# Causal attention: mask and row maximum of the scores in one VectorE call per head and query chunk, with a mask row over all keys

## The chip, the cores and the metric

The kernel runs on one core of a Trainium2 chip. The metric is device time in microseconds (us) of one execution of the whole program, lower being better. The engines are named as in the profile: PE (TensorE matmuls), PEld (TensorE weight loads), DVE (VectorE), ACT (ScalarE), POOL (GpSimd), SP (SyncE, which issues the DMAs).

## The reference, cut to what matters

The program is a stack of six blocks on a tensor of 16 sequences x 512 positions x 256 channels: a quantised feed-forward block, a Mamba block, the feed-forward block again, a LoRA expert block, **causal attention with ALiBi**, and the LoRA block again. Only the attention is touched:

```python
q = (x @ Wq + bq).reshape(Bb, Ss, H, HD)          # 16 heads of 16
k = (x @ Wk + bk).reshape(Bb, Ss, H, HD)
v = (x @ Wv + bv).reshape(Bb, Ss, H, HD)
scores = jnp.einsum('bthd,bshd->bhts', q, k) / jnp.sqrt(jnp.asarray(HD, x.dtype))
scores = scores + alibi[None]
scores = jnp.where(causal[None, None], -jnp.inf, scores)
attn = jax.nn.softmax(scores, axis=-1)
out = jnp.einsum('bhts,bshd->bthd', attn, v).reshape(Bb, Ss, Dd)
return out @ Wo + bo
```

## The kernel before, in words

The attention computes every score twice. First with queries on the partitions, only to find each query's maximum (the "peak" pass); then with keys on the partitions and the maximum already subtracted, to exponentiate (the "weigh" pass). ALiBi and the subtracted maximum ride in extra rows of the 32-row operands `q` and `k` of a head, so both passes are matmuls of 32 rows.

The work is cut into 64 **units** (16 sequences b x 4 groups j of 4 heads), and a unit into 6 **steps** (part, pair): three parts of query chunks (chunk 3 of 512 keys; chunk 2 of 384 keys; chunks 1 and 0 together, of 256 and 128 keys) times two pairs of heads. I number them step 0 to step 5; steps 0 and 1 are part 0, steps 2 and 3 part 1, steps 4 and 5 part 2. The loop over units (from L1564) is a software pipeline: while unit A goes through its peak pass, unit C (the one before) goes through its weigh pass and unit Dn (two before) is multiplied with the values. In each step:

- `peak_score` (L1170) and `weigh_score` (L1215) put the matmuls on PE, in turns. The scores of A land in a PSUM tile `s` with tag `sp`, of which there are two: step n+2 writes where step n was read.
- `weigh_exp` (L1233): ACT exponentiates the scores of C, POOL zeroes the masked triangle.
- `peak_max` (L1186): DVE adds the mask to the diagonal blocks of both heads of the pair (L1192, one TENSOR_TENSOR in PSUM), and then takes the maximum over the keys of each query chunk for both heads (L1196, one TENSOR_REDUCE for a chunk: one in parts 0 and 1, two in part 2). Results go into columns of `mx`.
- In step 0 of the next unit `peak_rows` (L1201) lets PE transpose `mx` (four 128x128 transposes, recorded at L1068) and DVE adds the result to `q`, giving `qm` (L1212), which the weigh pass of that unit needs from step 1 on. Then PE does `apply` (matmuls `o`).
- Between the steps `aside` (L1328) slips in side work: the projections of the coming sequence (`project`, L1070: norm at L1091 to L1100, the key bias on DVE at L1131 as `ku`, the values at L1154 and the output bias at L1164), the division (L1273, L1274) and the output projection (`close`, L1304).

Matmuls and transposes of this phase are kept in program order on PE (`keep_in_program_order`, L1065 and L1068). The DVE instructions are not: a scheduler places them, with semaphores for what depends on what, so an edit can move neighbours of the edited instruction too.

The mask is a bf16 tile of 128 x 256, two copies of one 128 x 128 triangle (L1037 to L1044), built once, before the first unit.

Of the kernel before, what the change touches and what calls it, by code (L numbers as in the profile page):

```python
# [10 lines left out]
BF16 = mybir.dt.bfloat16  # L11
AF = mybir.ActivationFunctionType
ALU = mybir.AluOpType
AX = mybir.AxisListType
PSUM = bass.MemoryType.PSUM

P = 128
NB, SEQ, D = 16, 512, 256
# [12 lines left out]
NX = NE * NR + 1  # L31
EPS = 1e-5
MASKED = -1e30


@with_exitstack
def macaron_kernel(
# [31 lines left out]
    nc = tc.nc  # L69

    const = ctx.enter_context(tc.tile_pool(name="const", bufs=1))
# [869 lines left out]
    def attn_phase(weights, pre):  # L941
# [8 lines left out]
        RS, RM = HD, HD + 1  # L950
# [10 lines left out]
        PEAK = (((3, 0),), ((2, 0),), ((1, 0), (0, 2 * P)))  # L961
        WEIGH = ((0,), (1,), (2, 3))
        wp, qs, ks, mxs, vas, qms, const, pools = {}, [], [], [], [], {}, {}, {}

        def constants(aw):

            for name, w in (("q", Wq), ("k", Wk), ("v", Wv), ("o", Wo)):
                t = aw.tile([P, KD, D], F32, name=f"w{name}")
                nc.sync.dma_start(out=t, in_=w.rearrange("(k p) f -> p k f", p=P))
                wp[name] = t  # L970
            bvb = aw.tile([P, D], F32, name="bvb")
            nc.sync.dma_start(out=bvb, in_=bv.unsqueeze(0).to_broadcast([P, D]))
            bob = aw.tile([P, D], F32, name="bob")
            nc.sync.dma_start(out=bob, in_=bo.unsqueeze(0).to_broadcast([P, D]))

            yield
            bq_t = aw.tile([P, KD], F32, name="bq_t")
            nc.sync.dma_start(out=bq_t, in_=bq.rearrange("(k p) -> p k", p=P))
            nc.vector.tensor_scalar(bq_t, bq_t, 0.25, None, op0=ALU.mult)
            bk_t = aw.tile([P, KD], F32, name="bk_t")  # L980
            nc.sync.dma_start(out=bk_t, in_=bk.rearrange("(k p) -> p k", p=P))

            prow = aw.tile([P, 1], F32, name="prow")
            nc.gpsimd.iota(
                prow, pattern=[[0, 1]], base=0, channel_multiplier=1,
                allow_small_or_imprecise_dtypes=True,
            )
            for i in range(1, 4):
                rows = prow[32 * i : 32 * i + 32, :]
                nc.vector.tensor_scalar(rows, rows, -32.0 * i, None, op0=ALU.add)  # L990
            is_s = aw.tile([P, 1], F32, name="is_s")
            nc.vector.tensor_scalar(is_s, prow, float(RS), None, op0=ALU.is_equal)
            neg_m = aw.tile([P, 1], F32, name="neg_m")
            nc.vector.tensor_scalar(
                neg_m, prow, float(RM), -1.0, op0=ALU.is_equal, op1=ALU.mult
            )
            slope = aw.tile([P, NJ], F32, name="slope")
            for h in range(NH):
                i, j = h % 4, h // 4
                nc.vector.memset(  # L1000
                    slope[32 * i : 32 * i + 32, j : j + 1], 2.0 ** (-8.0 / NH * (h + 1))
                )
            nc.vector.tensor_scalar(slope, slope, is_s, None, op0=ALU.mult)
            pos = aw.tile([P, SEQ], F32, name="pos")
            nc.gpsimd.iota(
                pos, pattern=[[1, SEQ]], base=0, channel_multiplier=0,
                allow_small_or_imprecise_dtypes=True,
            )


            yield
            for i in range(2):
                for j in range(NJ):
                    qs.append(aw.tile([P, SEQ], F32, name=f"q{i}{j}"))
                    ks.append(aw.tile([P, SEQ], F32, name=f"k{i}{j}"))
            last = ks[-1]
            nc.vector.tensor_scalar(last, pos, 0.0, neg_m, op0=ALU.mult, op1=ALU.add)
            for c, i, row in BLOCKS:
                nc.vector.tensor_scalar(
                    last[:, P * c + 32 * i : P * c + 32 * i + 32],  # L1020
                    prow.to_broadcast([P, 32]), float(row), neg_m,
                    op0=ALU.is_equal, op1=ALU.add,
                )
            yield
            for i in range(2):
                for j in range(NJ):
                    nc.vector.tensor_scalar(
                        qs[i * NJ + j], pos, 0.0, is_s, op0=ALU.mult, op1=ALU.add
                    )
                    nc.vector.scalar_tensor_tensor(  # L1030
                        ks[i * NJ + j], pos, slope[:, j : j + 1], last,
                        op0=ALU.mult, op1=ALU.add,
                    )
                    yield


            mask = aw.tile([P, 2 * P], BF16, name="mask")  # L1037
            nc.vector.memset(mask, 0.0)
            for i in range(2):
                square = mask[:, i * P : (i + 1) * P]  # L1040
                nc.gpsimd.affine_select(
                    out=square, in_=square, compare_op=ALU.is_ge,
                    fill=MASKED, base=0, pattern=[[-1, P]], channel_multiplier=1,
                )  # L1044
            yield
            for r in range(3):
                if r < 2:
                    mx = aw.tile([P, NC4, 4, 32], F32, name=f"mx{r}")
                    nc.gpsimd.memset(mx, 0.0)
                    for c, i, row in BLOCKS:  # L1050
                        nc.gpsimd.memset(mx[: 32 * i, c, :, row : row + 1], MASKED)
                    mxs.append(mx)
                va = aw.tile([P, NC4, VW], F32, name=f"va{r}")
                nc.gpsimd.memset(va, 1.0)
                vas.append(va)
            const.update(
                bvb=bvb, bob=bob, bq_t=bq_t, bk_t=bk_t, mask=mask
            )
# [126 lines left out]

        def peak_max(b, j, part, pair, s):  # L1186
            mx = mxs[(b * NJ + j) % 2]
            t, off = PEAK[part][0]
            w = len(PEAK[part]) * P

            own = s[:, :, off + t * P : off + t * P + w]
            nc.vector.tensor_tensor(  # L1192
                own, own, const["mask"][:, :w].unsqueeze(1).to_broadcast([P, 2, w]), op=ALU.add
            )
            for t, off in PEAK[part]:
                nc.vector.tensor_reduce(  # L1196
                    mx[:, t, 2 * pair : 2 * pair + 2, RM],
                    s[:, :, off : off + (t + 1) * P], axis=AX.X, op=ALU.max,
                )

        def peak_rows(b, j):  # L1201

# [104 lines left out]
        with tc.tile_pool(name="aw", bufs=1) as aw:  # L1307
            with tc.tile_pool(name="a", bufs=2) as ap, tc.tile_pool(
                name="a_s", bufs=1, space=PSUM
# [237 lines left out]


                making = constants(aw)
                for _ in range(2):  # L1550
                    rows_of.append(ap.tile([P, 4, EW], F32, name="eT", tag="eT"))
# [12 lines left out]
                for u in range(len(units) + 2):  # L1564
# [16 lines left out]
                    for n, (part, pair) in enumerate(steps):  # L1581
# [15 lines left out]
                        if A:  # L1597
                            peak_max(*A, part, pair, sp)
# [39 lines left out]
    with tc.tile_pool(name="mw", bufs=1) as mw:  # L1638
        with tc.tile_pool(name="x", bufs=1) as xp, tc.tile_pool(
            name="fw", bufs=1  # L1640
# [23 lines left out]
    with tc.tile_pool(name="fw2", bufs=1) as fw, tc.tile_pool(  # L1664
        name="ln2", bufs=2
    ) as lnp:
        weights = []
        for i, d in enumerate(kept):
            w = fw.tile([P, d.shape[1], d.shape[2]], F32, name=f"wk{i}")
# [66 lines left out]
```

## Time and profile before

| what | value |
|---|---|
| median of 3 runs (lowest, highest) | 4259.38 us (4258.01, 4263.89) |
| span of the profiled execution, first to last instruction | 4259.0 us |
| busy over the span: PE, DVE, ACT, POOL | 92%, 88%, 54%, 44% |
| mask and maximum on DVE (first L1192 to last L1196) | from 3126.7 to 4127 us of the span |
| mask additions L1192 | 384 instructions, 199.0 us |
| maxima L1196 | 512 instructions, 410.2 us on the page (421.1 us with all forms told apart) |
| mean granted PE clock | 0.975 |

The span is the time of the profiled execution as far as the profile has it; it lies 0.4 us under the median of the runs. A row of instructions gives the line, engine and operation, the tiles written and read, the shape (partitions x elements), the count, the busy time in us, and the mean of one in ns. In a list by time, the first number is the start in us from the start of the span and the second the duration. Two VectorE instructions in a row with no semaphore between them can overlap in such a list, since a record runs from an instruction's start to the end of its last write. The chain of waits follows the last instruction of the span backwards: at each point it holds the instruction that everything after was waiting for.

### The profile page before, as it was taken

How to read it: one execution, taken by the hardware profiler on the slowest of the kernel's cores; microseconds unless marked ns; L12 is line 12 of the kernel's file. 1: busy time of each engine (PE TensorE's matmuls, PEld its weight loads, DVE VectorE, ACT ScalarE, POOL GpSimd, SP SyncE). 2: the span in 40 equal slices, each digit the busy share in tenths (PEclk: the TensorE clock that was granted, in tenths of full speed). 3: DMA queues.
4: the chain of work that ended last, by engine and by line, in shares of the span. 5: the costliest groups of instructions: out<-in, count | busy, mean ns of one | idle time of the engine just before them, and what ended most of it. 6: DMA issues, size and time to landing. Idle time of an engine off the chain costs nothing.

```text
span 4259.0 us, 50441 instructions
## 1 busy us (share of the span) xinstructions
PE 3903.6 (92%) x17986; PEld 2129.9 (50%) x17986; DVE 3751.8 (88%) x4970; ACT 2284.9 (54%) x3463; POOL 1877.2 (44%) x1653
## 2 busy tenths in 40 slices
PE   6999977988899888888888799999999999999989
PEld 4676632333333333333333366666755555555547
DVE  9999858999999999999999899998878888888766
ACT  4444336667767676676777344443524444444434
POOL 1000027888888898888988600000301111111121
PEclk9999999999999999999999999999999999999999
DMA  4000023444444444444443020000000000000002
GB/s 143 16 16 15 20 100 104 132 122 134 139 144 144 144 143 144 134 135 133 139 138 120 11 109 1 1 1 1 13 21 20 19 17 18 19 20 14 21 11 70
DMA packets 120605, 303.00 MB, mean 71 GB/s; under 512 B 25297, under 2 KB 45330, under 8 KB 103970
## 3 DMA queue, kind: packets, MB, share of 16 engines
q1 hardware_dynamic: 120354, 299.78, 22.4%
q8 instruction: 142, 2.33, 0.2%
q14 instruction: 109, 0.89, 0.1%
HBM read 238.63 MB, written 44.30 MB: 66 GB/s over the span
## 4 chain that ended last, share of the span: by engine, by line
PE 66%; DVE 14%; POOL 12%; ACT 5%; issue 2%; DMA 1%; SPq 0%; DVEq 0%; POOLq 0%; ACTq 0%
PE y L486 11%; PE s L1065 10%; PE g L288 7%; PE u L288 7%; POOL bx L480 7%; PE o L324 7%; PE p L486 5%; PE p L1065 4%; DVE h L876 4%; PE o L486 3%; PE p L1068 3%; PE o L1065 3%; POOL g L480 2%; PE r L1065 2%; DVE mx L1196 2%
## 5 line engine op out<-in xcount | busy, mean ns | idle before, releaser
L480 POOL TENSOR_TENSOR bx<-dtu,bc 128x1024 f32<-128x1024 f32 x512 | 1193.9, 2360 | 46.4 <-DVE h L876 46.3
L486 PE MATMUL y<-g,ident 128*128 128x512 f32 x2048 | 1008.9, 631 | 128.7 <-DVE g L483 128.6
L876 DVE TENSOR_TENSOR_SCAN h<-da,bx 128x1024 f32<-128x1024 f32 x384 | 879.8, 2291 | 67.8 <-ACT da L477 30.4
L477 ACT ACTIVATE da<-dt,a_neg 128x511 f32<-128x511 f32 x1024 | 702.9, 688 | 219.3 <-DVE hs L876 116.8
L486 PEld LDWEIGHTS y<-g,ident 128*128 128x128 f32 x2048 | 390.0, 199 | 711.4 <-issue 464.8
L1242 POOL TENSOR_SCALAR_AFFINE_SELECT eT<-eT 128x256 f32<-128x256 f32 (+1 forms) x384 | 189.0, 492 | 867.0 <-ACT eT L1236 867.0
L1236 ACT ACTIVATE eT<-s 128x768 f32<-128x768 f32 (+1 forms) x384 | 338.4, 881 | 422.1 <-PE s L1065 422.1
L483 DVE TENSOR_TENSOR g<-h,bc 128x1024 f32<-128x1024 f32 x384 | 468.9, 1221 | 28.2 <-PE o L486 0.5
L1065 PE MATMUL s<-k,q 32*128 32x256 f32 (+3 forms) x2048 | 458.2, 469 | 9.1 <-DVE mx L1196 5.7
L1196 DVE TENSOR_REDUCE mx<-s 128x2 f32<-128x1024 f32 (+3 forms) x512 | 410.2, 822 | 12.5
L1065 PE MATMUL s<-qm,k 32*128 32x512 f32 (+3 forms) x2048 | 385.5, 471 | 18.2 <-ACT eT L1236 11.8
L480 POOL TENSOR_TENSOR g<-hs,bc 128x1024 f32<-128x1024 f32 x128 | 301.6, 2356 | 156.8 <-DVE hs L876 140.8
L1192 DVE TENSOR_TENSOR s<-s,mask 128x256 f32<-128x256 f32 (+1 forms) x384 | 199.0, 518 | 155.7 <-PE s L1065 145.6
L293 ACT ACTIVATE sl<-g 128x352 f32<-128x352 f32 x256 | 118.1, 464 | 383.2 <-PE g L288 372.4
L876 DVE TENSOR_TENSOR_SCAN hs<-da,bx 128x1024 f32<-128x1024 f32 x128 | 292.0, 2281 | 2.5 <-ACT da L477 2.5
L1065 PEld LDWEIGHTS s<-k,q 32*128 32x128 f32 x2048 | 205.7, 184 | 172.2 <-issue 93.8
L1393 POOL TENSOR_TENSOR g<-rs,v 128x4 f32<-128x4 f32 x64 | 13.1, 208 | 631.8 <-ACT rs L1390 548.8
L486 PE MATMUL p<-xT,w_in 128*128 128x512 f32 x500 | 242.1, 607 | 20.9 <-ACT xT L477 10.1
L509 POOL MEMSET xs<- 128x12 f32 x2 | 0.2, 110 | 532.7 <-DMA xd<-x 532.7
L477 ACT ACT_TABLE_LOAD x170 | 218.1, 1283 | 3.0
L1065 PEld LDWEIGHTS s<-qm,k 32*128 32x128 f32 x2048 | 170.1, 185 | 63.9 <-ACT eT L1236 34.7
L288 PE MATMUL g<-wgT,xT 128*128 128x352 f32 x512 | 183.7, 469 | 0.0
(270 smaller groups left out, 6766.6 us busy)
## 6 DMA issues: line engine op xcount, KB each, us to landing
bc<-bd SPq DMA_DIRECT2D x128, 1024.0 KB, 6.3
xs<-xc SPq DMA_DIRECT2D x240, 256.0 KB, 4.7
xc<-xp SPq DMA_DIRECT2D x60, 256.0 KB, 2.0
x<-_attn_hidden_states_dram SPq DMA_DIRECT2D x16, 512.0 KB, 6.6
xd<-x SPq DMA_DIRECT2D x16, 512.0 KB, 2.6
xo<-xd SPq DMA_DIRECT2D x16, 512.0 KB, 3.6
xe<-xo SPq DMA_DIRECT2D x16, 512.0 KB, 2.6
x<-xe SPq DMA_DIRECT2D x16, 512.0 KB, 10.7
```

The lines of the kernel that those rows point to most:

```text
L288: nc.tensor.matmul(dst, lhsT=xT[:, k, c * P : (c + 1) * P], rhs=w[:, k, f0 : f0 + HF], start=(k == 0), stop=(k == KD - 1),)
L324: last = nc.tensor.matmul(o, lhsT=hT[:, f, :], rhs=wdT[:, f, :], start=(f == 0), stop=False)
L477: return tc.keep_in_program_order(nc.scalar.activation(out, in_, func, **kw))
L480: tc.keep_in_program_order(nc.gpsimd.tensor_tensor(out, in0, in1, op=op))
L483: tc.keep_in_program_order(nc.vector.tensor_tensor(out, in0, in1, op=op))
L486: tc.keep_in_program_order(nc.tensor.matmul(out, **kw))
L876: tc.keep_in_program_order(nc.vector.tensor_tensor_scan(flat(h), flat(das[t % 2]), flat(bxs.pop(t)), 0.0, op0=ALU.mult, op1=ALU.add,))
L1065: tc.keep_in_program_order(nc.tensor.matmul(out, **kw))
L1192: nc.vector.tensor_tensor(own, own, const["mask"][:, :w].unsqueeze(1).to_broadcast([P, 2, w]), op=ALU.add)
L1196: nc.vector.tensor_reduce(mx[:, t, 2 * pair : 2 * pair + 2, RM], s[:, :, off : off + (t + 1) * P], axis=AX.X, op=ALU.max,)
L1236: const["exp"] = nc.scalar.activation(eT[:, 2 * pair : 2 * pair + 2, e0 : e0 + w], s[:, :, :w], AF.Exp)
L1242: nc.gpsimd.affine_select(out=own, in_=own, compare_op=ALU.is_ge, fill=0.0, base=0, pattern=[[0, 2], [0, n], [1, P]] if n > 1 else [[0, 2] ...
```

## The change

The mask becomes one bf16 row block of 128 x 512: zero everywhere but in the last 128 columns, which hold the triangle. For a chunk of w keys the last w columns are used, so that the triangle meets the diagonal block. For each head and chunk one call, `tensor_tensor_reduce`, adds the mask to all w scores, multiplies by 1.0, writes the row back and puts the maximum, started from -3e38, into `mx`. Before, a step had one mask addition and one or two reduces, each over two heads; now it has two or four calls, each over one head.

```diff
-            mask = aw.tile([P, 2 * P], BF16, name="mask")
+            mask = aw.tile([P, SEQ], BF16, name="mask")
             nc.vector.memset(mask, 0.0)
-            for i in range(2):
-                square = mask[:, i * P : (i + 1) * P]
-                nc.gpsimd.affine_select(
-                    out=square, in_=square, compare_op=ALU.is_ge,
-                    fill=MASKED, base=0, pattern=[[-1, P]], channel_multiplier=1,
-                )
+            nc.gpsimd.affine_select(
+                out=mask[:, SEQ - P :], in_=mask[:, SEQ - P :],
+                compare_op=ALU.is_ge, fill=MASKED, base=0, pattern=[[-1, P]],
+                channel_multiplier=1,
+            )
...
         def peak_max(b, j, part, pair, s):
             mx = mxs[(b * NJ + j) % 2]
-            t, off = PEAK[part][0]
-            w = len(PEAK[part]) * P
-
-            own = s[:, :, off + t * P : off + t * P + w]
-            nc.vector.tensor_tensor(
-                own, own, const["mask"][:, :w].unsqueeze(1).to_broadcast([P, 2, w]), op=ALU.add
-            )
             for t, off in PEAK[part]:
-                nc.vector.tensor_reduce(
-                    mx[:, t, 2 * pair : 2 * pair + 2, RM],
-                    s[:, :, off : off + (t + 1) * P], axis=AX.X, op=ALU.max,
-                )
+                w = (t + 1) * P
+                for i in range(2):
+                    row = s[:, i, off : off + w]
+                    nc.vector.tensor_tensor_reduce(
+                        row, row, const["mask"][:, SEQ - w :], 1.0, LOWEST,
+                        op0=ALU.add, op1=ALU.max,
+                        accum_out=mx[:, t, 2 * pair + i, RM : RM + 1],
+                    )
```

More of the change, by code (lines that the diff above doesn't have):

```diff
@@ L33 @@
 MASKED = -1e30
+LOWEST = -3e38
 @with_exitstack
```

## The prediction

> **What bounds the kernel now.** I first read the busy times by stretch (engines in the order PE, PEld, DVE, ACT, POOL; busy us and instructions):
>
> ```profile
> core 0: us, PE busy (x) PEld busy (x) DVE busy (x) ACT busy (x) POOL busy (x), PEclk, DMA share, GB/s
> 3500.00:3700.00 200.00, 194.68 (x1553) 101.28 (x1552) 164.06 (x302) 87.92 (x118) 38.38 (x78) 0.99 0.08 19
> ```
>
> In the attention PE is busy 97% of the time and DVE 82%. So PE is the bound, and time taken from DVE counts only where PE waits for DVE. The groups by line and shape give the prices:
>
> ```profile
> L1196 DVE TENSOR_REDUCE mx<-s 128x2 f32<-128x1024 f32 x128 | 156.4, 1222 | 3.8
> L1196 DVE TENSOR_REDUCE mx<-s 128x2 f32<-128x768 f32 x128 | 122.7, 959 | 4.4
> L1192 DVE TENSOR_TENSOR s<-s,mask 128x256 f32<-128x256 f32 x256 | 109.7, 429 | 132.1 <-PE s L1065 127.3
> L1192 DVE TENSOR_TENSOR s<-s,mask 128x512 f32<-128x512 f32 x128 | 89.3, 697 | 23.6 <-PE s L1065 18.3
> L1131 DVE TENSOR_SCALAR ku<-p,bk_t 128x512 f32<-128x512 f32 x32 | 23.8, 742 | 0.2 <-PE p L1065 0.2
> L1000 DVE MEMSET slope<- 32x1 f32 x16 | 0.9, 59 | 0.6
> ```
>
> To see where PE waits I compared, for all 64 units, the end of a unit's last maximum with the start of the transposes of `mx` (L1068). Of every four units of a steady sequence,
> - two have the key projection `ku` at their end (28 such units in all): transposes start 0.21 us after the last maximum, with PE busy until then;
> - one has the value projection (14 units): transposes start 0.05 us after it, and PE has idled 0.78 us: DVE sets the end;
> - one has the next norm (14): 1.12 us after it; DVE becomes late a little later, through norm and `qm`.
>
> So 0.05 us is the bare signal, and a `ku` unit has 0.21 - 0.055 = **0.155 us of slack**. A `ku` unit's end on DVE, in order of time:
>
> ```profile
> 3322.66 0.70 DVE L1192 TENSOR_TENSOR s<-s,mask 128x512 f32<-128x512 f32 x1
> 3323.39 1.02 DVE L1196 TENSOR_REDUCE mx<-s 128x2 f32<-128x512 f32 x2
> 3324.34 0.74 DVE L1131 TENSOR_SCALAR ku<-p,bk_t 128x512 f32<-128x512 f32 x1
> 3324.99 0.42 DVE L1192 TENSOR_TENSOR s<-s,mask 128x256 f32<-128x256 f32 x1
> ```
>
> The maximum needs the addition and starts 0.03 to 0.04 us after its end. Instructions that wait for nothing on DVE overlap: two maxima of 693 and 416 ns take 1.02, not 1.11, and `ku` starts 0.07 to 0.09 before their end. I use **+0.04 us for a wait on DVE itself, -0.085 us without one**. The chain of waits at the end of a value unit:
>
> ```profile
> 3427.66 0.98 PE s L1065 x9
> 3428.63 0.02 issue
> 3428.66 0.71 DVE s L1192
> 3429.37 0.02 issue
> 3429.39 1.02 DVE mx L1196 x2
> 3430.42 0.60 DVE va L1154
> 3431.01 0.60 DVE x L1164
> 3431.61 0.62 DVE s L1192
> 3432.23 0.02 issue
> 3432.26 1.03 DVE mx L1196 x2
> 3433.29 0.04 issue
> 3433.33 0.66 PE p L1068 x4
> ```
>
> From scores to transposes everything is DVE: 3428.66 to 3433.29, 4.63 us.
>
> **What the change does.** The changed program's order of instructions shows two things that the diff hides. First, each call becomes **two** DVE instructions: the row operation (R) and a second one without input that writes one value per partition into `mx` (A). 896 instructions become 2048. Each R of a step but the first waits for the A before it, since both write `mx`. Second, **neighbours move**. In 28 units `ku` is now ahead of the last R of step 5 (R A R A R A ku R A); before, it came behind the last maximum. In 14 value units `va` and `x` stand among the calls of step 4. PE, ACT and SP keep their order; POOL loses one affine select.
>
> **Price of R.** The addition L1192 reads the same PSUM scores and the same bf16 mask and writes PSUM. 697 - 429 = 268 ns for 256 elements is 1.047 ns an element, so R is 697 (512), 563 (384), 429 (256) and 295 ns (128). Its result is a running maximum, like L1196's, whose rows have the same slope. The other end: the scan L876, which carries a value along too, takes 2291 ns for 1024, twice as much an element. I take the first: addition and maximum alone each run at it.
>
> **Price of A.** No row shows it. Call e the time from R's end to A's end. The nearest row is the MEMSET: no input, one element per partition, 59 ns. Placed as instructions without a wait are, 0.085 before R's end, it gives e = -25 ns; placed at R's end, e = 60; as an instruction of the smallest size with input (about 160 ns), starting 36 ns behind R's end as the MEMSETs do behind each other (14 in 1.29 us), e = 195. I take **e = 60**, between these and nearest to the MEMSET, and keep -25 to 195.
>
> The Trainium skill speaks against the change here. "VectorE: DVE Perf Modes", Rules for kernel authors, says not to fuse chained DVE operations but to lower their number, semaphores not mattering, since each pays its flush. The trace disagrees about semaphores (0.04 against -0.085 us), and agrees that the number counts. With that page's measured fixed term of 151 cycles, 157 ns, for each A the sum below would be an estimate of +50 us, 4309.
>
> **The sum, by kind of unit** (ns, e left open):
> - **`ku` units, 28.** Step 5 had 1760 from its first instruction to its last end (3322.66 to 3324.42). Now: R 429 + 429 + 295 + 295 = 1448; four A: 4e; two self-waits 80; `ku` between: 742 - 85 behind it, less 40 for its own overlap with A = 617. Together 2145 + 4e, later by 385 + 4e, less the slack 155: **230 + 4e**. At e = 60: 470 ns x 28 = **+13.2 us**. Above e = 88, step 4 also pushes: it takes 1568 + 4e, step 5 starts 40 ns ahead of its end, and the two starts are 1.88 us apart now (3320.78 to 3322.66, set by PE): 4e - 350 more. PE has no other work there: the transposes stand in its queue ahead of `apply`, and this stretch of the chain is PE, so a stall is lost time.
> - **Value units, 14.** Steps 4 and 5 with `va` and `x`: R 2 x 1448 = 2896; `va` and `x` 600 each as now; 8e; four self-waits 160; three overlaps behind an A, -120. 4136 + 8e against 4620: **-484 + 8e**, at e = 60 -4 ns, **0.0 us**. Step 4's buffer comes free 1.2 us later, but the scores waiting for it (1.07 us of PE) still end ahead of the transposes, in the 0.78 us that PE idles: nothing.
> - **Norm units, 14.** Chain: step 5, norm, step 0, `qm`. Step 5: 1448 + 4e + 80 - 1760 = -232 + 4e (one self-wait is filled by L1091). Step 0: 2 x 697 + 2e against 1.60: -206 + 2e. **-438 + 6e**, at e = 60 -78 ns, **-1.1 us**.
> - Steps 1 to 3, and step 0 elsewhere: DVE gains or loses beside a busy PE, which covers it; nothing, unless DVE fills up (it has 12.6 us in a unit of 15.4: 82% of a quarter of 61.66 us, one sequence, from 3310.01 to 3371.67). If that cover went, a step of part 0 would gain 1691 - 1394 - 40 - 2e = 137 ns at e = 60.
> - The mask is built beside busy PE before the first unit: a memset twice as long (165 ns now), one affine select (328 ns) less: nothing, at most 0.2 us.
>
> Sum at e = 60: 13.2 + 0.0 - 1.1 = **+12.1 us**. Span 4259.0 + 12.1 = 4271.1; the runs' median lies 0.4 above the span: **4271.5 us**. With e open: -6.5 us + 0.308e, plus 28 x (4e - 350) above 88.
>
> **Rivals.**
> - *Faster: A hides in R's tail.* For it: unwaited pairs overlap 85 ns, and A has no wait. Against: A needs R's last element. At e = -25 value units gain 0.68, norm units 0.59 us, and `ku` units lose only 0.13: -14.2 us, 4245. It decides from e = 21 down; beyond 0.2% (8.5 us) from e = -7.
> - *Small either way:* e from -7 to 49, 4251 to 4268. For it: DVE handles 768 elements a head pair in part 2 and 1024 in part 0 where it handled 1280.
> - *A is a full, separate instruction:* e = 100 to 195, +26 to +66 us, 4285 to 4325; of the last, `ku` units are 40 us, value units 15, norm units 10. For it: A writes another memory than R and comes after a result that is final only with R's last element.
> - *R at the scan's rate:* 5120 elements a unit x 1.04 ns = 5.3 us more DVE in a unit; 12.6 - 9.2 (masks and maxima, start to start) + 8.9 (16 R and A) + 5.3 = 17.6 against 15.4: DVE becomes the bound, 2.2 x 64: about +140 us.
> - *The change doesn't do what it says* (one instruction): it doesn't, by the order; that is e. Should the chip delay `ku` less than the order says, 28 x 0.617 at most, 17 us, come off: the faster side again.
>
> **How the numbers follow.** Forecast (e 49 to 100): 0.40. Small either way: 0.20. Faster by over 0.2%: 0.18. Separate A: 0.17. Scan rate: 0.05. The two last together with the forecast are slower by over 0.2%: 0.62. 0.2% is about what a measurement of this kernel can tell from no change. The range reaches from e = -25 to e = 195, 4245 to 4326; only the scan rate, and what I have not thought of, lie outside.
>
> **What would show it.** A row L1192 with a second group without input, 128x1, x1024, whose mean is A; R near 697 and 429 ns; DVE busy lower by about 50 us (620 to 508 + 61) and yet a longer time; transposes of `mx` starting 0.05 instead of 0.21 us after the last A in `ku` units, PE idle about 0.5 us ahead of them; value units unchanged. Wrong if A starts ahead of R's end, if R has another fixed part than L1192, or if `ku` units lose nothing.

## The result and the profile after

The changed kernel takes **4275.9 us** (median of 5 runs, 4270.6 to 4278.7) against 4258.6 us (4257.1 to 4263.9) for the kernel before: ratio **1.0039**, 95% interval 1.0028 to 1.005. It is slower, by 17 us. The profiled execution took 4275.9 us, its span 4274.2 us (the kernel before: 4259.0).

The busy times of the same stretch as in the prediction (us, then PE, PEld, DVE, ACT and POOL):

```profile
3500.00:3700.00 200.00, 189.19 (x1532) 98.70 (x1525) 151.39 (x527) 85.30 (x114) 36.59 (x75) 0.98 0.07 17
```

DVE has 12.7 us less to do in these 200 us, and over the whole span 3700.6 us instead of 3751.8. Yet PE, the bound, is busy 189.2 and not 194.7 us: it now waits more, so less gets done. The groups by line and shape show the new instructions:

```profile
L1192 DVE CUSTOM_DVE_ANT_0 s<-s,mask 128x512 f32<-128x512 f32 x256 | 179.9, 703 | 120.2 <-PE s L1065 116.4
L1192 DVE DVE_READ_ACCUMULATOR2_ANT mx<- 128x1 f32 x1024 | 144.9, 142 | 0.0
L1192 DVE CUSTOM_DVE_ANT_0 s<-s,mask 128x256 f32<-128x256 f32 x256 | 111.3, 435 | 40.5 <-PE s L1065 32.7
L1192 DVE CUSTOM_DVE_ANT_0 s<-s,mask 128x128 f32<-128x128 f32 x256 | 75.9, 296 | 6.0
```

One call is two instructions: R (the CUSTOM rows, at the old addition's rate) and A (the READ_ACCUMULATOR row, one value per partition). On DVE, in order of time, the last step of a `ku` unit is now:

```profile
3327.59 0.43 DVE L1192 CUSTOM_DVE_ANT_0 s<-s,mask 128x256 f32<-128x256 f32 x1
3327.94 0.14 DVE L1192 DVE_READ_ACCUMULATOR2_ANT mx<- 128x1 f32 x1
3328.11 0.43 DVE L1192 CUSTOM_DVE_ANT_0 s<-s,mask 128x256 f32<-128x256 f32 x1
...
3328.86 0.14 DVE L1192 DVE_READ_ACCUMULATOR2_ANT mx<- 128x1 f32 x1
3329.04 0.75 DVE L1131 TENSOR_SCALAR ku<-p,bk_t 128x512 f32<-128x512 f32 x1
3329.71 0.29 DVE L1192 CUSTOM_DVE_ANT_0 s<-s,mask 128x128 f32<-128x128 f32 x1
3329.92 0.14 DVE L1192 DVE_READ_ACCUMULATOR2_ANT mx<- 128x1 f32 x1
```

`ku` stands ahead of the last pair, and the step takes 2.47 us (3327.59 to 3330.06) where it took 1.76. The transposes start at 3330.11, 0.05 us after the last A, and PE has idled 0.48 us. An A starts 0.083 us before its R ends and ends 0.059 us after it (medians of all 1024; 0.057 to 0.060); where the next R waits for the A, it follows 0.035 us behind.

**Where the 15.2 us of span come from.** I measured every unit from the transposes of `mx` to the next transposes, in both traces, and took the median by kind over the steady part, some 3200 to 4020 us, which is also where halved stretches are counted below (a unit's late gain in norm and `qm` shows in the unit after it). Separately I summed (1 - granted PE clock) from 3120 to 4200 us of the one profiled execution of each kernel; the last column is the difference of the medians of all its runs. The table gives the differences to the kernel before for all kernels of this study; the rows below the first are the experiments.

| kernel | first ku, norm, second ku, value unit (us) | 14 x their sum | clock lost (before: 22.2 us) | median less that of before |
|---|---|---|---|---|
| after | +0.55, 0.00, +0.20, -0.21 | +7.7 | 29.0 | +17.3 |
| e1_ku_behind | 0.00, +0.18, -0.35, -0.02 | -2.6 | 18.8 | -5.9 |
| e2_old_ku_ahead | +0.50, 0.00, +0.50, -0.01 | +13.9 | 34.1 | +22.9 |
| e3_new_parts01 | 0.00, 0.00, -0.19, 0.00 | -2.8 | 18.8 | -5.6 |
| e4_new_part2 | +0.55, 0.00, +0.40, -0.21 | +10.5 | 25.6 | +21.7 |
| e5_junk | 0.00, 0.00, -0.51, -0.85 | -19.0 | 15.4 | -23.5 |
| e6_pe_filled | +0.96, -0.06, +0.61, -0.26 | +17.5 | 30.7 | +23.3 |
| e7_old_ku_ahead_filled | +0.97, -0.06, +0.97, -0.06 | +25.5 | 25.6 | +37.8 |
| e8_fill_ku | +0.56, 0.00, +0.20, -0.21 | +7.7 | 23.9 | +15.6 |
| e9_fill_ku_value | +0.55, 0.00, +0.20, -0.21 | +7.7 | 17.1 | +8.2 |
| e10_before_fill_value | 0.00, 0.00, 0.00, -0.01 | -0.1 | 22.2 | +2.3 |

So 7.7 us are longer units, as the prediction had it in kind, and 6.8 us (29.0 - 22.2) are something that it did not have: stretches in which **PE's granted clock is halved** (six in the steady part, two in the kernel before). One of them, behind the end of a value unit, in three windows of 3.4 us (the last three columns are PEclk, DMA share, GB/s):

```profile
3562.30:3565.70 3.40, 1.85 (x27) 1.22 (x20) 3.30 (x15) 1.46 (x2) 0.64 (x1) 1.00 0.02 5
3565.80:3569.20 3.40, 3.40 (x23) 0.91 (x25) 1.49 (x5) 0.06 (x1) 0.64 (x1) 0.50 0.00 0
3569.20:3572.60 3.40, 3.40 (x41) 2.05 (x36) 1.42 (x5) 1.94 (x3) 0.26 (x1) 1.00 0.00 0
```

In the first window PE idles 1.55 us; the whole next one runs at 0.50, with 23 matmuls where the third has 41; then the clock is back. That costs 1.6 to 1.7 us: a first `ku` unit that holds such a stretch takes 16.81 to 16.88 us and not 15.18. The idle time has two parts, seen on PE at the end of another value unit (the bracket is the idle time and its releaser):

```profile
3439.27 0.69 PE L1065 MATMUL s<-k,q 32*128 32x512 f32 x1 [1.00 <-DVE mx L1192]
...
3440.96 0.33 PE L1068 MATMUL p<-ident,mx 128*128 128x128 f32 x1 [0.56 <-DVE mx L1192]
```

The 0.56 us stood at 0.78 before:

```profile
3433.33 0.66 PE L1068 MATMUL p<-ident,mx 128*128 128x128 f32 x4 [0.78 <-DVE mx L1196]
```

The 1.00 us is new (0.07 before): these scores go into step 4's buffer, which now comes free only after `va` and `x`.

### The profile page after: what moved, and what is told of

Read it like the earlier page. It is cut to its first block, busy times and chain, and to the rows that moved or that the text cites. A ratio compares the mean times of both kernels' runs of the same rounds, so it can differ in the third digit from the quotient of the medians.

```text
span 4274.2 us, 51571 instructions
## 1 busy us (share of the span) xinstructions
PE 3897.8 (91%) x17986; PEld 2124.7 (50%) x17986; DVE 3700.6 (87%) x6122; ACT 2285.4 (53%) x3463; POOL 1874.4 (44%) x1652
## 3 DMA queue, kind: packets, MB, share of 16 engines
q1 hardware_dynamic: 120354, 299.78, 22.2%
## 5 line engine op out<-in xcount | busy, mean ns | idle before, releaser
L1192 DVE CUSTOM_DVE_ANT_0 s<-s,mask 128x512 f32<-128x512 f32 (+3 forms) x1024 | 506.6, 500 | 231.0 <-PE s L1065 209.0
L1065 PE MATMUL s<-k,q 32*128 32x256 f32 (+3 forms) x2048 | 448.4, 471 | 20.8 <-DVE mx L1192 20.7
L1065 PEld LDWEIGHTS s<-qm,k 32*128 32x128 f32 x2048 | 170.7, 186 | 50.8 <-ACT eT L1233 25.5
L289 PE MATMUL g<-wk,xT 128*128 128x352 f32 x512 | 183.9, 469 | 0.6 <-DMA wk<-wd 0.6
```

Source lines behind the costliest of these rows:

```text
L289: nc.tensor.matmul(dst, lhsT=xT[:, k, c * P : (c + 1) * P], rhs=w[:, k, f0 : f0 + HF], start=(k == 0), stop=(k == KD - 1),)
L1065: tc.keep_in_program_order(nc.tensor.matmul(out, **kw))
L1192: nc.vector.tensor_tensor_reduce(row, row, const["mask"][:, SEQ - w :], 1.0, LOWEST, op0=ALU.add, op1=ALU.max, accum_out=mx[:, t, 2 * pair ...
```

## The experiments

My theory after the trace: the loss is `ku` ahead of the last pair, made worse by R's wait for A; the clock loss follows from PE's idle time. Rivals: the A instructions cost the same wherever they stand; the clock is all of it.

**ku put back (e1_ku_behind).**

```diff
-    nc.vector.tensor_scalar(r, p, bk_t[:, m : m + 1], None, op0=ALU.add)      # ku, L1131
+    with tc.issue_after(const.get("peak", const["exp"]).ins):                 # peak: the newest R
+        nc.vector.tensor_scalar(r, p, bk_t[:, m : m + 1], None, op0=ALU.add)
...
-                    nc.vector.tensor_tensor_reduce(
+                    const["peak"] = nc.vector.tensor_tensor_reduce(
```

> The changed kernel, with the key bias ku issued behind the last accumulator read of step 5, where the old kernel had it; nothing else moves. Theory (the moved neighbour): step 5 of a ku unit takes about 1.79 us against 1.76 before, inside the 0.155 us of slack, so the 0.55 us stalls of the ku units go; value units keep their gain of 0.21 us and norm units theirs of 0.35: about 4259 - 14 x 0.56 = 4251 us, and the transposes of a ku unit start 0.15 to 0.21 us after the last read, with PE busy until then. Rival 1 (the 1024 added accumulator reads cost wherever they stand): stays at 4270 or more. Rival 2 (the added stretches of half clock are the cost, whatever the order): falls by less than 6 us, to about 4270.

4251.5 us against 4257.4: ratio 0.9987 (0.9978 to 0.9996). With `ku` behind, the loss is gone: the new call by itself is no slower. The expected 4251 us was met partly by luck: the units gain only 2.6 us and not 7.8, since the value units' 0.21 us did not show, and the profile lost 3.4 us less clock than that of the kernel before (18.8 against 22.2). The chain of waits at the end of a `ku` unit has something new:

```profile
3689.37 0.66 PE p L1068 x4
3690.03 0.11 issue
3690.14 2.36 PE o L1065 x32
```

`apply` starts 0.11 us late, with nothing of its own missing (in the kernel before it follows the transposes at once). I read it as a wait for the PSUM buffer that `ku` reads and now frees later; against the kernel before it makes some 0.18 us a `ku` unit, 5 us in all. No run tried this by itself.

**The old calls with ku ahead (e2_old_ku_ahead).** The kernel before, with the last maximum of step 5 kept back and issued after `ku`; nothing of the new call.

```diff
         def peak_max(b, j, part, pair, s):
...
             for t, off in PEAK[part]:
+                if t == 0 and pair == 1 and j % 2 == 0:
+                    const["late"] = (mx, s, off, const.get("ku"))
+                    continue
...
+        def last_max():                       # the kept maximum, issued after the new ku
...
                             aside((4 if n == 1 else 3) if A else 5, n == 5)
+                        if "late" in const:
+                            last_max()
```

> The old kernel (mask addition and two-head maximum), with ku issued ahead of the last maximum of step 5, where the change put it. Theory (the moved neighbour): step 5 ends 0.65 us later, less 0.155 us of slack: 0.5 us x 28 = +14 us, 4273, without any of the new instructions; PE idles about 0.5 us ahead of the transposes of ku units. Rival 1 (the accumulator reads): 4259, unchanged. Rival 2 (clock): more stretches of half clock than the old kernel if PE's idle time is what brings them; then 4273 plus some 1.7 us for each.

4280.3 us, ratio 1.0059 (1.0046 to 1.0071). DVE at the end of a `ku` unit:

```profile
3330.05 0.74 DVE L1131 TENSOR_SCALAR ku<-p,bk_t 128x512 f32<-128x512 f32 x1
3330.71 0.41 DVE L1209 TENSOR_REDUCE mx<-s 128x2 f32<-128x256 f32 x1
```

A moved neighbour alone does it: +0.50 us in each of the 28 units, 13.9 us in all, as worked out; the remaining 9 us of the median go with 11.9 us more clock lost in the profile. So the accumulator reads are not needed for the loss, and the clock is not all of it.

**The new call in some parts only (e3_new_parts01, e4_new_part2).** e3 uses it for parts 0 and 1 and keeps the old addition and reduces in part 2; e4 the other way round. The mask row has 640 columns, so that it holds both forms.

```diff
         def peak_max(b, j, part, pair, s):
+            if part == 2:      # e4: part < 2
+                (the old addition and reduces)
+                return
```

> The new call in parts 0 and 1 only (512 of the 1024), the old addition and maxima in part 2; ku stands behind the last maximum as in the old kernel. Theory: value and ku units as before, norm units gain 0.2 us in step 0: 4259 - 3 = 4256 us. Rival 1 (the reads cost wherever they stand): half of the 17 us, 4267.

> The new call in part 2 only (512 of the 1024), the old addition and maximum in parts 0 and 1; ku stands ahead of the last call of step 5, as in the changed kernel. Theory: ku units lose 28 x 0.55 = 15.4 us, value units gain 14 x 0.21 = 2.9, norm units 14 x 0.15 = 2: +10.5 us and some 5 of half clock: 4274 us. Rival 1 (the reads cost wherever they stand): half of the 17 us, 4267.

e3: 4251.7 us, ratio 0.9985 (0.9976 to 0.9994). e4: 4279.1 us, ratio 1.0049 (1.0037 to 1.0062). 512 of the 1024 pairs, in parts 0 and 1, cost nothing and gain a little through step 0 and `qm`; the whole loss is in part 2. The rival that a pair costs wherever it stands falls. Both medians miss what was expected (4256 and 4274) by 4 to 5 us, though the units do what was expected of them (-2.8 and +10.5 us). In e3 the profile lost 3.4 us less clock than that of the kernel before; e4's profile is its fastest run (4271.1 us), so its 25.6 us of lost clock need not stand for the others.

**R's row to a scratch (e5_junk).** Nothing reads the masked scores, so R may write them elsewhere.

```diff
+                    jk = ap.tile([P, SEQ], BF16, name="jk", tag="jk", bufs=2)
                     nc.vector.tensor_tensor_reduce(
-                        row, row, const["mask"][:, SEQ - w :], 1.0, LOWEST,
+                        jk[:, :w], row, const["mask"][:, SEQ - w :], 1.0, LOWEST,
...
-            oT = ap.tile([P, SEQ], F32, name="oT", tag="oT")
+            oT = ap.tile([P, SEQ], F32, name="oT", tag="oT", bufs=1)
```

The second change makes room: `oT`, the division's copy of `o` (not the output bias, as the expectation has it), has one buffer and not two.

> The changed kernel, with the row operation writing its masked scores into a rotating bf16 scratch (two buffers in SBUF) instead of back into the PSUM scores; the output bias tile oT has one buffer less to make room. Nothing reads the masked scores, so the output is the same. A row operation then waits on the one two before it and no longer on its predecessor's second instruction, and ku, va and x stand behind the steps again. My theory (the loss is ku's place and the waits on DVE itself, each costing about 0.12 us against an instruction without a wait): step 5 takes about 1.3 us and not 1.76; value units get 0.78 us shorter until PE sets their end, norm units 0.35 to 0.6, ku units 0.0 to +0.2 (ku frees its PSUM buffer later); -13 to -19 us in all, 4240 to 4246, faster than both kernels, with no more half-clock stretches than before. Rival (the second instruction holds the next row operation back whether it waits or not): no gain beyond putting ku behind, 4249 to 4254. Rival (the read of PSUM with a write to SBUF is slower than in place): step 5 no shorter than 1.76 us, 4258 or more.

4234.4 us (5 runs, 4230.3 to 4237.4) against 4257.9: ratio **0.9945** (0.9933 to 0.9958), faster than both kernels and by more than the 4240 to 4246 expected: the units give -19.0 us, the lower end of what was expected, and the profile lost 6.8 us less clock. Groups, DVE at the end of a `ku` unit, and the busy times of the stretch:

```profile
L1193 DVE CUSTOM_DVE_ANT_0 jk<-s,mask 128x256 bf16<-128x256 f32 x256 | 98.3, 421 | 73.9 <-PE s L1065 73.9
L1193 DVE DVE_READ_ACCUMULATOR2_ANT mx<- 128x1 f32 x1024 | 84.7, 83 | 0.0
```

```profile
3415.78 0.08 DVE L1193 DVE_READ_ACCUMULATOR2_ANT mx<- 128x1 f32 x1
3415.78 0.42 DVE L1193 CUSTOM_DVE_ANT_0 jk<-s,mask 128x256 bf16<-128x256 f32 x1
3416.13 0.08 DVE L1193 DVE_READ_ACCUMULATOR2_ANT mx<- 128x1 f32 x1
...
3416.65 0.75 DVE L1131 TENSOR_SCALAR ku<-p,bk_t 128x512 f32<-128x512 f32 x1
```

```profile
3500.00:3700.00 200.00, 198.01 (x1599) 103.79 (x1598) 139.41 (x549) 91.23 (x122) 38.74 (x81) 1.00 0.09 21
```

Now the next R starts in the same moment as the A before it: a pair of 256 takes 0.35 us (3415.78 to 3416.13), in the changed kernel 0.52 (3327.59 to 3328.11). Step 5 takes 1.20 us. Without R's waits the scheduler leaves `ku`, `va` and `x` behind the steps. PE is busy 198 of 200 us, no stretch of halved clock falls into the steady part, and value units lose their 0.78 us of idle time. The kernel differs from e1 in more than R's wait: R is 10 to 17 ns shorter, but the 14 R on the paths of a value and a norm unit make some 0.2 us by estimate, and a sequence of four units is 1.2 us shorter than in e1. So most of it is the wait and the order of the neighbours that comes with it; the two were not taken apart. The rivals (the next R held back by A anyway; a slower write to SBUF) fall.

**Does PE's idle time halve the clock?** First I filled PE's gap ahead of the transposes in `ku` units with a matmul whose result the transposes overwrite, in the changed kernel (e6) and in e2 (e7):

```diff
             p = ps.tile([P, SEQ], F32, name="p", tag="mm")
+            if j % 2 == 0:
+                matmul(p, lhsT=ident, rhs=wp["v"].rearrange("p k d -> p (k d)"), start=True, stop=True)
             for t in range(NC4):
```

> The changed kernel with one more matmul (128x512, identity times the value weights) put on PE ahead of the transposes of mx in the units that end with ku; the transposes overwrite its result, so it adds work that is not in the reference and changes no output. It needs nothing that DVE makes, so it fills most of the 0.5 us that PE idles there and moves no DVE work. Theory that the idle gaps bring the half-clock stretches (each about 1.7 us): the stretches fall from 11 to 9 or fewer of the same span, and the time from 4276 to 4266 to 4270, although PE has more to do. Rival (the half-clock stretches come at random or from other gaps, those in value units too): stretches stay at 10 to 14, 4275 to 4279. Rival (the added matmul delays the transposes): ku units 0.1 us or more longer still, 4279 or more.

> The kernel before with its last maximum of step 5 put behind ku in 29 units (as in the run before it of that kind, which took 4280 us with 14 half-clock stretches) and with the same added matmul ahead of the transposes as in the run beside this one (its result is overwritten). Theory that PE's idle gaps bring the half-clock stretches: the 14 us of stall stay, the 12 us of stretches go mostly: 4267 to 4272, 10 stretches or fewer. Rival (stretches do not depend on these gaps): 4279 to 4283, 13 to 15 stretches.

4281.3 us, ratio 1.0056 (1.0043 to 1.0069), and 4295.8 us, ratio 1.0091 (1.0076 to 1.0106). The filler was too large: it runs as two matmuls, 0.96 us in place of the 0.48 or 0.43 of idle time, so each `ku` unit grew by 0.41 to 0.47 us. As a test of the clock they fail; but 5 stretches stayed in the steady part of e6, where after has 6, though the `ku` gaps were full. Where stretches start in the steady part is telling: always at whole multiples of 3.413 us from one another, and behind the gaps of value units or a wait of 0.53 us for ACT in part 1 of the second `ku` unit (the expectations below put it into step 0, wrongly), never behind the gap ahead of a `ku` unit's transposes. So I halved the filler (0.43 us) and put it into `ku` units (e8), into value units as well (e9: `j != 1`), and into value units of the kernel before (e10: `j == 3`):

```diff
+            if j % 2 == 0:
+                matmul(p[:, : 2 * P], lhsT=ident, rhs=wp["v"][:, 0], start=True, stop=True)
```

> The changed kernel with an added matmul of half the width of the last filler (256 columns, 0.43 us of PE in its two halves) ahead of the transposes in units that end with ku only; the transposes overwrite its result, so it is work that the reference does not have. It fits into the 0.48 us that PE idles there, so the transposes should start when they did. In the profiles so far the half-clock stretches all last 3.40 to 3.45 us, begin at whole multiples of 3.413 us from one another, and in the changed kernel follow stretches of 3.4 us in which PE idles 1.55 us at the end of a value unit, or 0.53 us in step 0; none follows a ku unit's own gap. Theory that a fixed window with too much idle time halves the next one: filling the ku gaps changes nothing, 4273 to 4279 (5 stretches or so in the steady part). Rival (the ku gaps bring the stretches): fewer than 3 in the steady part, 4266 to 4271.

> The same with the added matmul in the value units too, where it takes 0.43 of the 0.56 us that PE idles ahead of the transposes, so that no window of 3.4 us there has 1.55 us of idle time but 1.1 at most. Theory (the window's idle time decides): the stretches after value units go, two or fewer are left in the steady part, and the median falls by 3 to 6 us against the run beside it that fills the ku units only: 4269 to 4273. Rival (the stretches do not depend on the idle time of these windows): as that run, within 2 us.

> The kernel before with the same added matmul (0.43 us, overwritten by the transposes) in its value units, where PE idles 0.78 us ahead of the transposes; nothing else is changed. Theory (a window with 0.78 us of idle time halves the next one): the 2 stretches of the steady part go, and the median falls by 2 to 5 us, 4253 to 4256. Rival: the stretches stay and the time does too, 4257 to 4260.

e8: 4273.1 us, ratio 1.0037 (1.0023 to 1.0051); e9: 4265.7 us, ratio **1.0019** (1.001 to 1.0028); e10: 4259.9 us, ratio 1.0005 (0.9996 to 1.0013). The units of after, e8 and e9 are alike to 0.01 us; the steady part has 6, 5 and 1 stretches. e9 does strictly more matmul work than e8 and is 7.5 us faster (3 to 6 were expected):

```profile
3500.00:3700.00 200.00, 195.32 (x1558) 102.48 (x1556) 151.77 (x528) 86.93 (x116) 37.33 (x77) 0.99 0.07 17
```

This splits the loss: about 8 us (e9's +8.2) are longer units, about 7.5 (e8 less e9) are the clock, brought on by the idle time ahead of a value unit's transposes and not by that of `ku` units. In the kernel before, the same filler gains nothing, so my theory for e10 missed: the two halved stretches behind value units went (one behind the wait for ACT came), but the median did not fall. Nor did the theory behind e9, that the idle time in a window decides, come out; the last section has the windows.

## Why the prediction was right, and where its terms were not

The time (4271.5 predicted) is right, in part by luck: value and norm units gained 6.7 us more than the terms had, and the clock lost about 7 that no term had. The mechanism of the largest term, `ku` ahead of the last pair, is right. By its steps:

- **Price of R: right.** 703, 566, 435 and 296 ns measured against 697, 563, 429 and 295. The scan rival falls.
- **Price of A: right in what counts.** e = 59 ns against 60. But not as a 59 ns instruction behind R's end: it is 142 ns, of which 83 lie in R's tail. "Wrong if A starts ahead of R's end", one of the prediction's own signs, came true without changing e, so the agreement of e is partly luck as well. The rival "A is separate" (e from 100) falls, "A hides in R's tail" as well, in this kernel.
- **Why R waits: wrong reason.** I put it to both writing `mx`. It is the write-back to the scores tile: in e5, with `mx` as it was and the row elsewhere, the wait is gone.
- **ku units: right, a little small.** 230 + 4e is 466 ns at e = 59; measured 0.55 us, +15.4 us for 28. Most of the rest is one overlap: `ku` does not overlap the A before it; it starts 0.04 us behind (3329.04), where I took 40 ns off. Transposes 0.05 us after the last A and PE idle 0.48 us came as forecast.
- **Value and norm units: the mis-sized term.** I took 40 ns off behind an A that the next instruction doesn't wait for. The trace has that instruction start together with A, so such an A costs nothing:

```profile
3438.26 0.14 DVE L1192 DVE_READ_ACCUMULATOR2_ANT mx<- 128x1 f32 x1
3438.26 0.69 DVE L1164 TENSOR_TENSOR x<-x,bob 128x512 f32<-128x512 f32 x1
```

 Value units: -0.21 us measured, -0.01 by -484 + 8e at e = 59. Norm units: `qm` starts 0.35 us earlier after the transposes, -0.08 by -438 + 6e; it shows in the second `ku` unit (0.55 - 0.35 = 0.20). Together -7.8 us where these terms give -1.3. Measured sum 15.4 - 7.8 = 7.6 us; predicted +12.1.
- **The term that is missing: the clock.** "Step 4's buffer comes free 1.2 us later ... nothing" holds for the unit: PE gets the buffer 0.93 us later (1.00 us of idle time against 0.07), and the scores still end ahead of the transposes. But the idle time ahead of the transposes, which I called free, brings halved stretches: about 7 us, in no term of the sum. e9 against e8 shows it. That the new 1.00 us has a part in it is not shown: e2, with the old calls and without it, lost 11.9 us more clock than the kernel before, and e1, which has it, 3.4 us less.
- **The DVE total: right.** Busy 51 us less, and a longer time: DVE's share was never the price; its order was.

## What to carry to other kernels

Before fusing operations on an engine that feeds the bound, count the instructions that the fused call becomes and see whether each waits for the one before: a result written back in place can cost 0.17 us a call (0.52 against 0.35 us), and a scratch output nobody reads can turn a loss of 0.4% into a gain of 0.55%. Look at what the scheduler moves between them: with the neighbours left in place the new instructions cost nothing here (e1), and one neighbour of 0.75 us ahead of the last instruction cost 0.59% by itself, some two fifths of it by the clock as far as the profile shows (e2). And idle time of the bounding engine that seems free in the sum may cost clock: here filling one gap of 0.56 us a sequence with useless work made the kernel 7.5 us faster (e9 against e8).

## What the runs showed of the hardware

**Halved PE clock in fixed windows.** Between 3120 and 4200 us of all twelve traces the stretches last 3.41 us or a multiple (up to 13.65), and those of one execution start on one grid of 3.413 us: in after, five of them lie 146.8, 126.3, 167.25 and 146.75 us apart, which is 43, 37, 49 and 43 windows, and all twelve stretches of after fit the grid within 0.02 windows. Cut by this grid, what matters at a value unit is where the window lies. In the nine traces with the gap of 0.56 or 0.78 us ahead of the transposes (all but e5, e9 and e10), every window of the steady part that starts 2.64 to 3.40 us ahead of them was followed by a halved one: 26 windows in seven traces. e1 and e3 have no window there, and no halved stretch in the steady part. No window that starts 2.61 us ahead or less, or 3.52 or more, was. Where the gap is gone or filled (e5, e9, e10), ten windows lie in the same place and none was followed by a halved one. The idle time in the window does not decide: a window of the kernel before with 0.78 us is followed by a halved one, one of e9 with 0.99 us, in nearly the same place, is not.

```profile
3553.90:3557.31 3.41, 2.63 (x20) 1.39 (x24) 3.34 (x7) 1.61 (x2) 1.08 (x2) 1.00 0.02 5
3557.31:3560.72 3.41, 3.41 (x25) 1.06 (x28) 1.49 (x2) 0.00 (x0) 0.23 (x1) 0.50 0.00 0
...
3312.00:3315.41 3.41, 2.42 (x26) 1.43 (x18) 3.31 (x16) 1.62 (x2) 0.68 (x2) 1.00 0.02 5
3315.41:3318.82 3.41, 3.41 (x42) 1.28 (x41) 1.32 (x4) 0.59 (x1) 0.60 (x1) 1.00 0.00 0
```

The first two lines are the kernel before, the last two e9. Whether a value unit is hit thus depends on how the loop's length fits the window: a sequence of four units is 18.013 windows long in e1, so the grid hardly moves against it, and 18.226 in after, so the window's place differs from one sequence to the next. With one profiled execution a kernel, this does not say why after loses more clock than the kernel before in the medians too; that stays open.

The Trainium skill ("TensorE: Matmul & The Clock Gate", Part 1) has a free-running window of 4096 cycles, 3413 ns, which the measured grid agrees with. Its rule there, no idle gaps over about 3.4 us, would not have been enough here: a gap of 0.78 us in a window was followed by half clock. What exactly is measured stays open, also because some windows with only the 0.53 us wait for ACT were followed by a halved one (two of after's, one of e9's), and others with as much were not.

**A read of the accumulator is short or long.** It takes 142 ns behind an R that writes PSUM and 83 ns behind one that writes bf16 to SBUF, ending 0.059 and 0.008 us after R's end. Where the next instruction does not wait for it or for another engine, it starts with the read in both cases (as at 3438.26 and 3415.78 above).
